# Two graph-attention layers and a transformer block on one core: first clips beside first values, ACT first at the values' banks, buffers of s moved, keys stacked inside SBUF, first rows loaded ahead of weights

## The chip, the cores and the metric

The kernel runs on one core of a Trainium2 chip. The metric is device time in microseconds (us); lower is better. Five runs of the kernel before gave a median of 3483.48 us (3477.29 to 3486.34).

The core's engines each take their instructions in a fixed order and wait for one another through semaphores: PE (matrix multiply; PEld is its weight load), DVE (vector), ACT (activation functions and copies), POOL (a second, slower vector engine) and SP, which here only issues transfers (DMA). The order on each engine is settled when the program is compiled.

## The reference, cut to what matters

There are 4096 rows of 256 features, 8 heads of 32, and a 4096x4096 adjacency matrix of int32.

```python
def _gat_layer(x, adj_mat, W, a):            # twice, each followed by elu(...) + input
    Wh = jnp.einsum('nd,hdo->hno', x, W)
    src = jnp.einsum('hno,ho->hn', Wh, a[:, :O])
    dst = jnp.einsum('hno,ho->hn', Wh, a[:, O:])
    e = jax.nn.leaky_relu(src[:, :, None] + dst[:, None, :], 0.2)
    e = jnp.where(adj_mat[None, :, :] > 0, e, NEG_INF)
    out = jnp.einsum('hnm,hmo->hno', jax.nn.softmax(e, axis=-1), Wh)
# then one transformer block with the same mask:
q, k, v = layer_norm(x) @ w_qkv              # split, 8 heads of 32
attn = softmax(where(adj != 0, q k^T * SCALE, -inf))
x = x + (attn v) @ w_proj + b_proj
x = x + gelu(layer_norm(x) @ w1 + b1) @ w2 + b2
```

## The kernel before, in words

**Graph attention** (`graph_attention`). exp(leaky_relu(s+d)) is either of two products of a row factor and a column factor, according to the sign of s+d. So the kernel only needs, per head, a 0/1 matrix "s >= -d" masked by the adjacency, and multiplies it by the values with their factors. The rows s are cut into 4 blocks of 1024. Work goes in 256 groups (layer, block of rows, pair of heads, group g of four 128-column tiles), 128 matmuls each at line 1302. For group i the loop over groups issues on PE the matmuls of group i, and beside them, at fractions of the group given by hand, the side steps of later groups:

- `compare(i + 2)`: eight comparisons of 128x1024, on DVE (line 1068) or on ACT (line 1066), then one AND with the mask on DVE (line 1073). The rows s come broadcast over the partitions in `s_b` (pool `g_s`, two buffers of 8 KB per partition), loaded by `s_fetch` (line 1049) from DRAM, where `term_rows` has put them (line 1019).
- For the mask of layer 0: `mask_load` fetches 512 KB of adjacency (line 855, three buffers), `mask_clip` turns it to fp8 on DVE (line 864, six buffers, and then issues the next load), `mask_turn` transposes it on PE (line 886), copies it out on ACT (line 888) and stores it (line 891).
- `preparation(l, q, bank)`: eleven steps for four tiles of values: two `features` (transposes at line 961, copies on ACT at line 964), then `values(t)` for t = 0 to 3, each followed one step later by `split(t - 1)`, and `term_rows`. `values` multiplies on PE (line 974) into a PSUM bank; DVE copies the 16 columns of terms (line 981); ACT takes two exponentials and a third one from that copy (lines 987, 988); DVE reduces (line 989), multiplies (line 995) into `g_prod` (two buffers) and scales (line 1001). `split` casts `g_prod` to f16 on ACT (line 1006) and POOL takes the remainder (line 1007).

Layer 0's eight preparations run in `begin()` (q = 0 and 1) and in groups 0 to 5; layer 1's run around groups 122 to 132. PE, ACT and DVE keep the written order inside this function (`manual_schedule`); SP's order is set by the planner. `begin()` runs preparation 0 and 1, with the first four clips beside q = 1, fetches s, then turns eight units and clips eight more, the last four of them for group 0's turns, and then compares for groups 0 and 1:

```python
        for q in range(2):
            for k, step in enumerate(preparation(0, q, spare_bank)):
                step()
                if q == 1 and k in (2, 4, 6, 8):
                    mask_clip(*units[k // 2 - 1])
```

**Pools.** A pool takes the addresses after those of the pools opened before it, and a pool opened after others are closed lies on their addresses and waits for whatever last used them. In order, after the masks (`g_mask`): `g_stage` 8 KB per partition, `g_rows` 26 KB, `g_t` 24 KB (the three compare buffers, read by the matmuls of line 1302 to the end), `g_s` 16 KB, `g_ep`. The transformer's pools lie on the same addresses: worked out from the tile sizes, counted from the end of `g_mask`, `u_mask` ends at 13 KB, `u_wq` is at 13 to 19 KB, `u_x` at 19 to 27, the layer norm's tiles (`u_ln`) at 27 to 37, its columns (`u_lnc`) at 37 to 45, the halves (`u_hv`) at 45 to 57.

**Queries, keys, values** (`unshifted_transformer`, line 1502). Eight blocks of 512 rows. `ready(nb)` loads rows (line 742) and normalises them (`normed`: mean on DVE at 1401, squares and a root on ACT at 1406 and 1410, rows on DVE at 1414); `turned` transposes them (PE line 1430, ACT line 1433). PE multiplies keys, then queries; ACT casts to f16 (line 1509), DVE takes the remainder (line 1510). The two halves go to `half_d` in DRAM in two stores (line 1514), and one block later come back in four loads (line 1455) as the stacked keys `u_k`, where partition group a of 32 holds half `order[a]` of head h in column h. Block 0's queries go the same way at once, those of later blocks while the attention runs. In this part all orders are the planner's, not written by hand.

**Attention** (lines 1554 to 1651) is scores on PE, exponential on ACT, mask on DVE, pair sums on POOL, and the products with values and ones on PE. Its last sums go through DRAM (`den_d`, `inv_d`, lines 1601 to 1623).

**Tail.** SP loads w_proj (line 1667), two row vectors (1671), w1 (1677) and w2 (1679), 1 MB each, and then `projected(0)` loads its rows (742) and its attention output (1692), adds the bias on POOL (1695), projects on PE (1699), adds on DVE (1706) and normalises. The feed-forward (1721, 1728, 1737) follows block by block, with `projected(nb + 1)` ahead of it.

Of the kernel before, what the change touches and what calls it, by code (L numbers as in the profile page):

```python
# [750 lines left out]
def graph_attention(  # L751
# [44 lines left out]
    mask_p = ctx.enter_context(tc.tile_pool(name="g_mask", bufs=10))  # L796
    stage_p = ctx.enter_context(tc.tile_pool(name="g_stage", bufs=2))
    rows_p = ctx.enter_context(tc.tile_pool(name="g_rows", bufs=2))
    t_p = ctx.enter_context(tc.tile_pool(name="g_t", bufs=3))
    s_p = ctx.enter_context(tc.tile_pool(name="g_s", bufs=2))  # L800
# [149 lines left out]
    def preparation(l, q, bank):  # L950
# [19 lines left out]
        def values(t):  # L970
# [10 lines left out]
            nc.vector.tensor_copy(  # L981
# [3 lines left out]
            big = some.tile([P, 2, H], F32, name="g_big")  # L985
            for i, scale in enumerate((-1.0, -LRELU)):
                nc.scalar.activation(big[:, i, :], L.negd[:, at, :], AF.Exp, scale=scale)
            nc.scalar.activation(L.r[:, at, :], L.terms[:, 0, at, :], AF.Exp, scale=LRELU - 1.0)
# [14 lines left out]
        def split(t):  # L1003
            part = held.pop(t).rearrange("p h i v -> p h (i v)")
            halves = vst[q][:, t].rearrange("p h (k v) -> p h k v", k=2)
            nc.scalar.copy(halves[:, :, 0, :], part)  # L1006
            nc.gpsimd.tensor_tensor(halves[:, :, 1, :], part, halves[:, :, 0, :], op=ALU.subtract)  # L1007
# [194 lines left out]
    def begin():  # L1202
# [5 lines left out]
        for q in range(2):  # L1208
            for k, step in enumerate(preparation(0, q, spare_bank)):
                step()  # L1210
                if q == 1 and k in (2, 4, 6, 8):
                    mask_clip(*units[k // 2 - 1])
        s_of[0, 0, 0] = s_fetch(0, 0, 0)
        for k, u in enumerate(units):
            mask_turn(*u)
            if k + 4 < len(units):
                mask_clip(*units[k + 4])
            else:
                mask_clip(*turns[0][k + 4 - len(units)])
# [110 lines left out]
def unshifted_transformer(  # L1330
# [42 lines left out]
    half_d = dram.tile([2, 2, DC, P, N], F16, name="half_d")  # L1373
# [69 lines left out]
    with ExitStack() as scope:  # L1443
# [7 lines left out]
        def stack(to, i, order, cols):  # L1451

            for a, kind in enumerate(order):
                first = half_d[i, kind, 0, 0:1, cols]
                nc.sync.dma_start(
                    to[a * O : (a + 1) * O],
                    spread(first, [[N, O], [O * N, DC * HC], [1, NB]]),
                )

        def load_queries(nb):  # L1460
            q_st = blocks.tile([P, DC * HC, NB], F16, name="u_q")
            stack(q_st, 0, (0, 1, 0, 1), slice(nb * NB, (nb + 1) * NB))
# [10 lines left out]
        with ExitStack() as qkv:  # L1473
# [16 lines left out]
            for nb in range(NNB):  # L1490
# [6 lines left out]
                for i in (1, 0):  # L1497
# [15 lines left out]
                    for kind in range(2):  # L1513
                        nc.sync.dma_start(
                            half_d[i, kind, :, :, cols].rearrange("c p n -> p c n"),
                            halves[:, kind],
                        )
# [11 lines left out]

                for b in (nb - 1,) if nb + 1 < NNB else (nb - 1, nb):  # L1530
                    if b >= 0:
                        at = slice(b * NB, (b + 1) * NB)
                        stack(k_st[:, :, at], 1, (0, 0, 1, 1), at)
                    if b == 0:
                        load_queries(0)
# [125 lines left out]
    with ExitStack() as scope:  # L1661
# [13 lines left out]
        b2_sb = by_row(b2, "u_b2")  # L1675
        w1_sb = big.tile([P, DC, F], F32, name="u_w1")
        nc.sync.dma_start(w1_sb, w1.rearrange("(c p) f -> p c f", p=P))
        w2_sb = big.tile([P, FC, D], F32, name="u_w2")
        nc.sync.dma_start(w2_sb, w2.rearrange("(c p) e -> p c e", p=P))
# [7 lines left out]
        def projected(nb):  # L1687

# [5 lines left out]
            )  # L1694
            nc.gpsimd.tensor_tensor(res, res, bp_sb, op=ALU.add)
# [15 lines left out]
        res, res_n = projected(0)  # L1711
        hn = turned(res_n, g2_sb, be2_sb, ln, ps_m)
        for nb in range(NNB):
            more = nb + 1 < NNB
            if more:
                res_next, res_n = projected(nb + 1)
# [115 lines left out]
```

## Time and profile before

| | us |
|---|---|
| median of five runs | 3483.48 |
| the profiled execution: its own time | 3481.72 |
| its span, first to last instruction | 3479.9 |
| start to the first matmul of group 0 | 61.35 |
| groups 0 to 5, about | 61 to 160 |
| layer 1's preparations, about | 896 to 975 |
| end of the last matmul of the graph attention | 1745.5 |
| first key matmul to first score matmul | 1761.87 to 1871.33 |
| end of the attention's last sums | 3185.6 |
| first feed-forward matmul | 3218.23 |

A line of the stage view gives, for a stretch of the span, its length, the busy time of each engine with the count of its instructions, the clock granted to PE as a share of full speed, the share of the DMA engines in use and GB/s. A line of the timeline gives start, length, engine, line, operation, output<-input and count; in brackets stands how long the engine was idle just before, and who ended that. A line of the waits gives the waiter, who released it, the total, the count and the longest. A line of one source line's instructions gives shortest/median/longest in ns. Times of consecutive instructions on DVE and ACT overlap by about 0.1 us, so that the step from one to the next is shorter than the length shown.

### The profile page before, as it was taken

The numbers are of one execution on the slowest core, as the hardware profiler recorded it, in microseconds if no ns is written. First come the engines' busy times: TensorE is split into PE (matmuls) and PEld (weight loads), VectorE is DVE, ScalarE is ACT, GpSimd is POOL, SyncE is SP. The second block draws the span as 40 slices with busy tenths as digits, with TensorE's granted clock in tenths as the row PEclk, the third lists the DMA queues.
The fourth block names the chain that finished last, engine by engine and source line by source line (L and its number), as shares of the span: only waits on it lengthen the run. The fifth ranks groups of instructions, "written<-read, shape, count | busy, mean of one in ns | idle before, by whom it ended". The sixth has DMA issues, their size and how long they took to land.

```text
span 3479.9 us, 97728 instructions
## 1 busy us (share of the span) xinstructions
PE 3299.2 (95%) x43156; PEld 2099.7 (60%) x43156; DVE 2882.0 (83%) x3250; ACT 2655.1 (76%) x3381; POOL 1323.1 (38%) x602
## 2 busy tenths in 40 slices
PE   4899999999889999999988999999999999997999
PEld 3799999999789999999953111111111111112666
DVE  6899999999779999999945999999999999996111
ACT  4799889988778888888855777777777777775332
POOL 1300000000210000000003999999999999996110
PEclk7999999999999999999989999999999999998999
DMA  6656545420311212121064010101011010002110
GB/s 203 189 183 203 157 152 163 142 81 27 96 51 39 74 47 87 39 75 39 13 177 113 19 31 19 32 25 25 25 26 37 13 44 10 26 10 67 44 47 26
DMA packets 214721, 250.57 MB, mean 72 GB/s; under 512 B 88528, under 2 KB 135632, under 8 KB 214288
## 3 DMA queue, kind: packets, MB, share of 16 engines
q1 hardware_dynamic: 214288, 244.25, 23.3%
q8 instruction: 339, 5.55, 0.6%
q14 instruction: 94, 0.77, 0.1%
HBM read 201.73 MB, written 42.47 MB: 70 GB/s over the span
## 4 chain that ended last, share of the span: by engine, by line
PE 39%; DVE 7%; ACT 4%; POOL 2%; DMA 1%; issue 1%; SPq 0%; DVEq 0%; ACTq 0%; POOLq 0%
PE u_ps L1554 12%; PE u_av L1568 12%; PE u_dn L1568 6%; DVE u_e L1563 4%; PE misc L1737 3%; PE bank L1302 2%; PE misc L1502 2%; POOL u_both L1651 2%; ACT u_ps L1561 1%; PE misc L1521 1%; PE misc L1721 1%; ACT ln_square L1406 1%; PE misc L1430 1%; DMA u_xres<-rows 1%; DVE t L1073 1%
## 5 line engine op out<-in xcount | busy, mean ns | idle before, releaser
L1302 PE MATMUL bank<-vst,t 128*128 128x66 f16 (+1 forms) x24576 | 1524.7, 203 | 47.4 <-DVE t L1073 39.9
L1302 PEld LDWEIGHTS <-t 128*128 128x128 fp8e4 x24576 | 1506.3, 97 | 66.6 <-DVE t L1073 48.5
L1302 PE MATMUL bank<-vst,mask 128*128 128x132 f16 x8192 | 1506.7, 222 | 0.0
L1066 ACT ACTIVATE t<-s_b,g_terms 128x1024 int8<-128x1024 f32 x1151 | 1243.5, 1164 | 99.2 <-PE bank L1302 94.7
L1651 POOL TENSOR_TENSOR u_both<-u_e 128x1024 f32<-128x1024 f32 x512 | 1199.9, 2366 | 233.1 <-DMA u_k<-half_d 126.4
L1563 DVE SCALAR_TENSOR_TENSOR u_e<-u_mask,u_ps 128x1024 f32<-128x1024 uint8 x1024 | 1202.4, 1217 | 88.5 <-ACT u_ps L1561 84.1
L1561 ACT ACTIVATE u_ps<-u_ps 128x1024 f32<-128x1024 f32 x1024 | 1010.9, 1008 | 281.4 <-PE u_ps L1554 262.4
L1302 PEld LDWEIGHTS <-mask 128*128 128x128 fp8e4 x8192 | 804.1, 98 | 0.0
L1073 DVE TENSOR_TENSOR t<-t,mask 128x2048 int32<-128x2048 int32 x256 | 589.9, 2304 | 110.7 <-ACT t L1066 89.3
L1068 DVE TENSOR_SCALAR t<-s_b,g_terms 128x1024 fp8e4<-128x1024 f32 x897 | 636.6, 754 | 0.0
L1554 PE MATMUL u_ps<-u_q,u_k 128*128 128x512 f16 x2048 | 579.6, 384 | 17.8 <-DVE u_e L1563 17.3
L1554 PEld LDWEIGHTS <-u_k 128*128 128x128 f16 x2048 | 139.2, 98 | 723.4 <-issue 664.3
L1568 PE MATMUL u_av<-u_e,u_v 128*32 128x512 f32 x4096 | 547.4, 606 | 0.0
L1007 POOL TENSOR_TENSOR vst<-g_prod,vst 128x528 f16<-128x528 f32 x64 | 83.9, 1321 | 937.8 <-ACT vst L1006 862.2
masks.py:197 POOL MEMSET u_ident<- 128x128 f32 x1 | 0.2, 205 | 727.5 <-ACT ln_square L1406 727.5
L1568 PE MATMUL u_dn<-u_both,u_ones 128*32 128x512 f32 x2048 | 274.1, 605 | 1.3 <-POOL u_both L1651 1.3
L1568 PEld LDWEIGHTS u_av<-u_e,u_v 128*32 128x32 f32 x4096 | 81.2, 108 | 219.1 <-issue 210.4
L1728 ACT ACTIVATE u_hid<-misc,u_b 128x512 f32<-128x512 f32 x64 | 42.3, 683 | 142.8 <-PE misc L1721 142.8
L1744 DVE TENSOR_TENSOR u_xres<-u_xres,misc 128x256 f32<-128x256 f32 x32 | 13.5, 421 | 122.7 <-PE misc L1737 122.7
L1737 PE MATMUL misc<-u_w,u_hid 128*128 128x256 f32 x512 | 111.8, 380 | 0.0
L1721 PE MATMUL misc<-ln_cols,u_w 128*128 128x512 f32 x256 | 111.2, 593 | 0.0
L864 DVE TENSOR_SCALAR adj<-g_adj 128x1024 fp8e4<-128x1024 int32 x128 | 97.2, 761 | 15.5 <-DMA g_adj<-in_adj_dram 15.5
(120 smaller groups left out, 1635.3 us busy)
## 6 DMA issues: line engine op xcount, KB each, us to landing
g_adj<-in_adj_dram SPq DMA_DIRECT2D x128, 512.0 KB
mask<-mask SPq DMA_DIRECT2D x128, 256.0 KB
s_b<-s_d SPq DMA_DIRECT2D x64, 512.0 KB
u_mask<-mask SPq DMA_DIRECT2D x32, 512.0 KB
mask<-stage SPq DMA_DIRECT2D x48, 256.0 KB
rows<-e_x SPq DMA_DIRECT2D x32, 256.0 KB
half_d<-u_halves SPq DMA_DIRECT2D x32, 256.0 KB
u_k<-half_d SPq DMA_DIRECT2D x32, 256.0 KB
```

Source lines behind the costliest of these rows:

```text
L864: nc.vector.tensor_scalar(v.rearrange("p m r -> p r m"), loaded.pop((nb, c, i)), 1.0, -(2.0**-30), op0=ALU.min, op1=ALU.max, saturate=False,)
L1066: nc.scalar.activation(to.bitcast(I8), s, AF.Sign, bias=negd, scale=-1.0)
L1068: nc.vector.tensor_scalar(to, s, negd, None, op0=ALU.is_ge, saturate=False)
L1073: nc.vector.tensor_tensor(both, both, m32.unsqueeze(1).to_broadcast(list(both.shape)), op=ALU.bitwise_and)
L1302: nc.tensor.matmul(to, left, right, start=k not in opened, stop=last)
L1554: nc.tensor.matmul(ps[:, j, :], k_st[:, h, mt * P : (mt + 1) * P], q_st[:, h, :], start=True, stop=True,)
L1561: nc.scalar.activation(ps, ps, AF.Exp, scale=SCALE)
L1563: nc.vector.scalar_tensor_tensor(e, mask, 0.0, ps, op0=ALU.not_equal, op1=ALU.mult)
L1568: nc.tensor.matmul(to[j * O : (j + 1) * O, :], lefts[j], es[j // 2][:, j % 2, :], start=start, stop=stop,)
L1651: nc.gpsimd.tensor_tensor(both, es_of[i - 1][u], es_of[i][u], op=ALU.add)
L1721: nc.tensor.matmul(ph, w1_sb[:, k, f * P : (f + 1) * P], hn[:, k, :], start=(k == 0), stop=(k == DC - 1),)
L1737: nc.tensor.matmul(po[:, :D], hid[:, f, at : at + P], w2_sb[:, f, :], start=(f == 0), stop=(f == FC - 1),)
```

## The change

Five edits:

1. `begin()`: clips of units 0 to 3 stand beside q = 0 (after steps 3, 5, 7, 9), clips of units 4 to 7 and the turns of units 0 to 2 beside q = 1; what follows turns units 3 to 7 and clips the four units of group 0.
2. `values` and `split`: the copy of the terms goes from DVE to ACT; the three exponentials read the PSUM bank and not the copy; `g_big` has four buffers; the cast in `split` goes from ACT to DVE.
3. The pool `g_s` is opened ahead of `g_stage`. Counted again from the end of `g_mask`: `g_s` 0 to 16 KB, `g_stage` 16 to 24, `g_rows` 24 to 50, `g_t` 50 to 74.
4. The halves of the keys, and of block 0's queries, go from SBUF to the stacked tile in SBUF, 16 transfers of 64 KB each per block (`stacked`), with no store to DRAM and no load from it. Later queries still go through `half_d`.
5. In the tail the rows and the attention output of block 0 are loaded before the second row vector, w1 and w2, and w_proj's tile is allocated after the first row vector.

```diff
     mask_p = ctx.enter_context(tc.tile_pool(name="g_mask", bufs=10))
+    s_p = ctx.enter_context(tc.tile_pool(name="g_s", bufs=2))
     stage_p = ctx.enter_context(tc.tile_pool(name="g_stage", bufs=2))
     rows_p = ctx.enter_context(tc.tile_pool(name="g_rows", bufs=2))
     t_p = ctx.enter_context(tc.tile_pool(name="g_t", bufs=3))
-    s_p = ctx.enter_context(tc.tile_pool(name="g_s", bufs=2))
...
-            nc.vector.tensor_copy(
+            nc.scalar.copy(
                 L.terms[:, :, at, :], pv[:, D : D + 2 * H].rearrange("p (k h) -> p k h", k=2)
             )
-            big = some.tile([P, 2, H], F32, name="g_big")
+            big = some.tile([P, 2, H], F32, name="g_big", bufs=4)
             for i, scale in enumerate((-1.0, -LRELU)):
-                nc.scalar.activation(big[:, i, :], L.negd[:, at, :], AF.Exp, scale=scale)
-            nc.scalar.activation(L.r[:, at, :], L.terms[:, 0, at, :], AF.Exp, scale=LRELU - 1.0)
+                nc.scalar.activation(big[:, i, :], pv[:, D + H : D + 2 * H], AF.Exp, scale=scale)
+            nc.scalar.activation(L.r[:, at, :], pv[:, D : D + H], AF.Exp, scale=LRELU - 1.0)
...
-            nc.scalar.copy(halves[:, :, 0, :], part)
+            nc.vector.tensor_copy(halves[:, :, 0, :], part)
             nc.gpsimd.tensor_tensor(halves[:, :, 1, :], part, halves[:, :, 0, :], op=ALU.subtract)
...
             for k, step in enumerate(preparation(0, q, spare_bank)):
                 step()
+                if q == 0 and k in (3, 5, 7, 9):
+                    mask_clip(*units[(k - 3) // 2])
                 if q == 1 and k in (2, 4, 6, 8):
-                    mask_clip(*units[k // 2 - 1])
+                    if k > 2:
+                        mask_turn(*units[k // 2 - 2])
+                    mask_clip(*units[k // 2 + 3])
         s_of[0, 0, 0] = s_fetch(0, 0, 0)
-        for k, u in enumerate(units):
-            mask_turn(*u)
-            if k + 4 < len(units):
-                mask_clip(*units[k + 4])
-            else:
-                mask_clip(*turns[0][k + 4 - len(units)])
+        for k in range(3, len(units)):
+            mask_turn(*units[k])
+            if k - 3 < len(turns[0]):
+                mask_clip(*turns[0][k - 3])
...
+        def stacked(to, halves, order):
+            for a, kind in enumerate(order):
+                by_chunk = to[a * O : (a + 1) * O].rearrange("p (c j) n -> p c j n", c=DC)
+                for j in range(HC):
+                    nc.sync.dma_start(by_chunk[:, :, j, :], halves[j * O : (j + 1) * O, kind])
...
-                    for kind in range(2):
-                        nc.sync.dma_start(
-                            half_d[i, kind, :, :, cols].rearrange("c p n -> p c n"),
-                            halves[:, kind],
-                        )
+                    if i == 1:
+                        stacked(k_st[:, :, cols], halves, (0, 0, 1, 1))
+                    elif nb == 0:
+                        load_queries(0, halves)
+                    else:
+                        for kind in range(2):
+                            nc.sync.dma_start(
+                                half_d[kind, :, :, cols].rearrange("c p n -> p c n"),
+                                halves[:, kind],
+                            )
...
-                for b in (nb - 1,) if nb + 1 < NNB else (nb - 1, nb):
-                    if b >= 0:
-                        at = slice(b * NB, (b + 1) * NB)
-                        stack(k_st[:, :, at], 1, (0, 0, 1, 1), at)
-                    if b == 0:
-                        load_queries(0)
...
         bp_sb = by_row(b_proj, "u_bp")
-        b2_sb = by_row(b2, "u_b2")
-        w1_sb = big.tile([P, DC, F], F32, name="u_w1")
-        nc.sync.dma_start(w1_sb, w1.rearrange("(c p) f -> p c f", p=P))
-        w2_sb = big.tile([P, FC, D], F32, name="u_w2")
-        nc.sync.dma_start(w2_sb, w2.rearrange("(c p) e -> p c e", p=P))
+        wp_sb = big.tile([P, DC, D], F32, name="u_wp")
+        nc.sync.dma_start(wp_sb, w_proj.rearrange("(c p) e -> p c e", p=P))
...
-        res, res_n = projected(0)
+        first = rows_of(0)
+        b2_sb = by_row(b2, "u_b2")
+        w1_sb = big.tile([P, DC, F], F32, name="u_w1")
+        nc.sync.dma_start(w1_sb, w1.rearrange("(c p) f -> p c f", p=P))
+        w2_sb = big.tile([P, FC, D], F32, name="u_w2")
+        nc.sync.dma_start(w2_sb, w2.rearrange("(c p) e -> p c e", p=P))
+        res, res_n = projected(*first)
```

`rows_of(nb)` holds the two loads that stood at the head of `projected`; later blocks call it just before `projected`.

## The prediction

> **What bounds the kernel now.** I read the page first, then a table of stages, then the waits and the timeline of the stages that the change touches.
>
> ```profile
> PE 3299.2 (95%) x43156; PEld 2099.7 (60%) x43156; DVE 2882.0 (83%) x3250; ACT 2655.1 (76%) x3381; POOL 1323.1 (38%) x602
> ```
>
> 95% of PE means that the long stages leave little. What can be won lies at the seams, so the next view is the table of stages (length, busy time per engine, clock, DMA share, GB/s):
>
> ```profile
> 0.00:61.30 61.30, 18.99 (x84) 13.68 (x84) 32.10 (x71) 24.57 (x56) 10.76 (x16) 0.73 0.72 226
> 61.30:160.00 98.70, 78.57 (x1038) 67.64 (x1039) 79.95 (x148) 67.43 (x164) 31.13 (x23) 0.96 0.54 168
> 896.00:975.00 79.00, 65.46 (x910) 56.97 (x911) 59.67 (x115) 57.66 (x142) 28.50 (x23) 0.98 0.31 96
> 1745.40:1761.90 16.50, 4.25 (x21) 3.17 (x18) 13.04 (x30) 12.32 (x29) 0.60 (x2) 0.60 0.67 208
> 1761.90:1871.30 109.40, 97.20 (x305) 57.32 (x305) 37.62 (x74) 54.50 (x132) 0.00 (x0) 0.92 0.64 170
> 3182.00:3218.20 36.20, 15.31 (x52) 10.72 (x49) 7.87 (x20) 7.88 (x15) 9.55 (x5) 0.67 0.49 160
> ```
>
> PE idles 42 us at the start, 20 and 14 in the two stretches of preparations, 12 at the change of layers, 12 in the key stage, 21 before the feed-forward. Every edit aims at one of these. Who ends the idle time, from the timeline (start, length, engine, line; in brackets the idle time before):
>
> ```profile
> 48.17 0.70 DVE L864 TENSOR_SCALAR adj<-g_adj 128x1024 fp8e4<-128x1024 int32 x1 [7.04 <-DMA g_adj<-in_adj_dram]
> 54.89 0.70 DVE L864 TENSOR_SCALAR adj<-g_adj 128x1024 fp8e4<-128x1024 int32 x1 [2.77 <-DMA g_adj<-in_adj_dram]
> 79.59 1.64 DVE L864 TENSOR_SCALAR adj<-g_adj 128x1024 fp8e4<-128x1024 int32 x1
> 89.27 0.69 DVE L995 TENSOR_TENSOR g_prod<-turn,g_big 128x512 f32<-128x512 f32 x1 [0.76 <-POOL vst L1007]
> 96.82 2.29 DVE L1073 TENSOR_TENSOR t<-t,mask 128x2048 int32<-128x2048 int32 x1 [1.25 <-ACT t L1066]
> 1745.51 1.22 DVE L1401 TENSOR_REDUCE ln_mean<-u_x 128x4 f32<-128x1024 f32 x1 [7.50 <-PE bank L1302]
> 1759.89 2.19 PE L1430 MATMUL misc<-u_ident,ln_rows 128*128 128x128 f32 x8 [3.68 <-DVE ln_rows L1414]
> 1811.75 2.19 PE L1430 MATMUL misc<-u_ident,ln_rows 128*128 128x128 f32 x8 [3.92 <-DVE ln_rows L1414]
> 3192.29 0.51 SPq L1692 DMA_DIRECT2D u_att<-att_d  x1
> 3197.92 6.04 PE L1699 MATMUL misc<-u_wp,u_att 128*128 128x256 f32 x16 [12.32 <-DMA u_att<-att_d]
> ```
>
> **Edit 1, clips.** A load needs the buffer of the third clip before it. Before, the first clip runs at 24.34, so DMA lies idle from 16 to 23 us, and clips 8 to 11 (counted from 0) wait for loads at 48.17 to 55.6; only then DVE does its five comparisons (3.4) and the AND (2.29): group 0 at 61.35. Now the first clip follows the second tile of values, at about 16.1. I follow DVE from 13.1 with steps of 1.0 for a tile, 0.6 for a clip, 0.35 for a cast and a wait for POOL (1.15 a tile) where `g_prod`'s two buffers are full: q = 0 ends at 25, q = 1 at 38, clip 8 runs at 39. Load 11, freed by it, took 6.0 before (issued about 48.9, clipped 54.89): clip 11 at 45.3, then 0.7 + 3.4 + 2.3: group 0 at 51.5. **-10 us.** Ends: the slowest load of this stretch (issue 39.26, clip 48.17: 8.9) with a slower DVE gives -5; no POOL waits gives -15. The fetch of s (8.4 from issue to landing) is no later: its terms now come from ACT, and it lands some 5 us ahead of clip 11. It is what is late next.
>
> **Edit 2, values.** Per group before, 16.4 us in layer 0 (83.34 to 99.70) and 13.4 in layer 1, set by DVE and ACT in turns. DVE loses four copies (0.09 each, start to start) and gains four casts of 128x528. No such cast is in the trace: ends are 0.35 (128x512 at 0.42, line 937, starts overlapping) and 0.63 (128x512 at 0.69, line 995); I take 0.35, since the 128x1024 comparison with one SBUF source also runs at that pace (0.75). So +1.0. ACT loses four casts (0.62) and gains four copies (0.17 to 0.25, as lines 988 and 1016): the wait at the AND goes (1.25 in layer 0; 0, 1.24, 2.49, 2.94 in layer 1, mean 1.7), with 0.17 in front of three products; PE's late banks (0.6 twice in layer 0) go about half. New: POOL now starts behind DVE's own cast, two steps before the next product needs the buffer: 0.8 and 0.9 of waiting instead of 0.76 (layer 0) and of 0.97 + 0.62 (layer 1). Sum: about -0.4 for 6 groups, -0.5 for 8: **-6 us.** Ends: casts at 0.63 add 14 x 4 x 0.28 = 16, so +10; no POOL waits at all, -17. The four `g_big` buffers are hidden: ACT runs at most that far ahead.
>
> A row speaks against this edit: the clip of 79.59 took 1.64, not 0.69, beside a POOL instruction, and POOL's own took 1.60, not 1.15. The Trainium skill, "SBUF — State Buffer", section "Who interferes with whom", has a rule for it: a cast or tensor_scalar in a two-port mode and a GpSimd instruction exclude each other for a whole instruction, while ScalarE never waits. By that rule at its worst each of the four casts brings one full POOL instruction into DVE's line, 4.6 per group where 2.7 are lost now; the sum of all edits would be -5 instead of -32.
>
> **Edit 3, places.** The layer norm's tiles lie at 27 to 37 KB: over `g_t`, read by the last matmul, before; over `g_rows`, long free, after. That is the 7.50 at 1745.51: DVE and ACT were idle from 1738. Now mean and squares of blocks 0 and 1 (2 x 1.2 on DVE, 2 x 2.5 on ACT) fit ahead of 1746. What stays: the constants (`u_eps`, g1, be1) lie over `g_keep`, last read by DVE at 1750.5 (line 1112); with no mean in its way that read ends at about 1749.2. Root, rows (1.4 a block), turns (2.2 a block, cold): keys start at about 1754.5 instead of 1761.87. **-7 us**; ends -11 (constants hidden too) and +2 (the planner leaves the means behind the GAT's tail). `u_wq` now waits for s, free at 1735; its 768 KB have 19 us. Without that cover it would cost its 3 to 4 us.
>
> **Edit 4, keys.** The trip through DRAM ends on no path: block 0's last load is issued at 1784.9, and scores start at 1871.33, 0.46 behind the copy of the last values. So 0 from the transfers. SP: 16 issues a block instead of 6. Nearest rows:
>
> ```profile
> L1455 SPq DMA_DIRECT2D u_k<-half_d x32: 444/462/493, 1772.6 to 1872.7; - x32
> L1514 SPq DMA_DIRECT2D half_d<-u_halves x32: 359/360/467, 1769.9 to 1868.8; - x32
> ```
>
> Issue to issue is 0.28 (line 1601, four in 1.12) to 0.50: 4.5 to 8.0 a block; with two query stores, rows and mask (1.7) at most 9.7, under the 11.2 of an unstalled block (1786.15 to 1797.35). Hidden. Block 0 has 32, 16 us at most: behind them the rows of block 4, now landed by 1775 and turned at 1796, would land at about 1787, and they need some 8 us to be normalised; it just fits. PE's stalls before blocks 5, 6 and 7 (3.92 each, plus 2.5 of slow clock) come from DVE's order: the mean at 1805.64 stands behind four remainders though its rows were issued at 1797.0. The planner may move it either way, 19 us for three blocks; nearest row: as before, 0.
>
> Against small transfers: the Trainium skill, "DMA: Bandwidth & Descriptors", section "Bandwidth", calls transfers under 64 KB descriptor-dominated and gives 0.95 us for 64 KB; sixteen in a row would be an estimated 15 us per block and PE would wait 4, which makes the sum about 0.
>
> **Edit 5, tail.** Before, SP meets the rows after w1, w2 and the wait for the sums (issue 3191.8), and `u_att` lands at 3197.8 among 2 MB of weights. After: four issues from 3182.0, done at 3183.9; 1.4 MB at the 0.3 to 0.38 MB/us of the start: 3188.5. **-9 us.** Ends: PE still warm (line 1699 takes 3.62 at 3246.65, not 6.04): -12; DVE's reciprocal of the sums (waiting until 3195.1) ordered ahead of the projections' additions: -2. The weights have from 3185 to 3209; what is late next is that chain of sums.
>
> **Sum.** -10 - 6 - 7 + 0 - 9 = -32. The profiled execution took 3481.7 (span 3479.9, 1.8 around it), so 3449.7; it lies 1.8 under the median, so **3451**.
>
> **Rivals.**
> - *The planner also frees blocks 5 to 7* (or most of edit 2's upper gain comes): 3451 - 19 = **3432**. For it: half a megabyte less traffic a block. Against: nothing in the diff moves the mean. 0.18.
> - *DVE becomes the bound of the preparations*: +10 in place of -6: **3467**. For it: the 1.64 and 1.60 rows. Against: DVE waits 2 to 4 us a group now. 0.17.
> - *The seams do not come*: the change doesn't do there what it says, because the planner keeps the old order (edits 3 and 5 give 0 and -2): **3465**. Against: both waits name a transfer or a buffer that is moved. 0.10.
> - *SP becomes the bound of the key stage.* 16 transfers at p plus 1.7 a block: the gains are eaten where a block takes (109.4 + 32) / 8 = 17.7, p = 1.0 us. At 1.13, the pitch of the four stores of line 1514 with their waits (4.52): 19.8 x 8 - 109.4 = +49, so **3500**. 0.07.
> - My forecast: 0.48; its own range is 3440 to 3462.
>
> 0.2%, about what a measurement can tell here, is 7 us. Faster: nearly all of the first four cases, 0.87; same 0.05 (DVE's bound with a stall or two); slower 0.08. The range 3426 to 3474 leaves out the SP case and the far end of the two before it.
>
> **What would show it.** Right: group 0's first matmul near 51; no clip waiting 7 us; the AND of a preparing group without a wait for ACT; the first mean ahead of the last matmul of the graph attention, and the first key matmul 9 us behind that matmul's end, not 16.4; 16 issues a block with SP idle between; the projection's 12.3 us wait down to about 3. Wrong: casts of 1 us or more on DVE; rows landing late in blocks 2 to 4; DVE's reciprocal ahead of the additions of line 1706.

## The result and the profile after

The changed kernel takes 3490.0 us (median of 23 runs, 3485.9 to 3494.2), the kernel before 3482.06 in the same comparisons: ratio 1.0022, 95% interval 1.0017 to 1.0028. It is slower by about 8 us, where 32 us less were forecast. The profiled execution took 3493.64, with a span of 3491.8. Line numbers are now each kernel's own: in the changed one they stand 2 to 17 higher from the main loop on.

The page of the changed kernel shows PE as busy as before, and ACT's work moved to DVE (2882.0 to 2904.6, ACT 2655.1 to 2622.7):

```profile
PE 3297.4 (94%) x43156; PEld 2100.3 (60%) x43156; DVE 2904.6 (83%) x3250; ACT 2622.7 (75%) x3381; POOL 1329.3 (38%) x602
```

The stages of the changed kernel, in the columns of the stage view: the start, layer 1's preparations, a stretch in the middle of layer 1 that was even before, the seam behind the graph attention, the key stage, the tail.

```profile
0.00:53.10 53.10, 17.19 (x85) 12.47 (x86) 32.36 (x71) 17.31 (x54) 12.17 (x16) 0.78 0.79 247
896.00:975.00 79.00, 66.04 (x969) 59.29 (x968) 68.64 (x119) 48.61 (x130) 29.96 (x20) 0.94 0.27 83
1213.00:1232.00 19.00, 11.86 (x208) 11.28 (x206) 9.22 (x11) 10.01 (x21) 0.00 (x0) 0.79 0.28 93
1748.40:1759.50 11.10, 2.54 (x10) 1.91 (x11) 9.12 (x24) 7.44 (x12) 0.60 (x2) 0.72 0.78 229
1759.50:1883.20 123.70, 98.04 (x313) 58.23 (x311) 39.26 (x76) 54.44 (x132) 0.00 (x0) 0.89 0.49 127
3198.30:3230.00 31.70, 15.93 (x53) 11.15 (x50) 9.46 (x20) 7.88 (x15) 9.53 (x5) 0.68 0.61 192
```

The start is 8 us shorter, the seam 5 and the tail 4, as planned in kind. The key stage is 14 longer with the same work on PE (98.04 against 97.20), and PE has a hole of 7 us near 1220, in a stretch where it did not wait at all before.

To see where each microsecond goes, I lined up the 256 AND instructions of the graph attention (DVE, line 1073, one per group), the first key matmul, the first score matmul, the start of the last pair sums on POOL and the end. After minus before, in us, in the two profiled executions:

| up to | running difference | step |
|---|---|---|
| AND of group 0 | -8.3 | -8.3 |
| AND of group 122 (layer 0's preparations done) | -10.1 | -1.8 |
| AND of group 160 (layer 1's preparations done) | -7.8 | +2.3 |
| AND of the last group | +2.5 | **+10.2** |
| first key matmul | -2.3 | -4.8 |
| first score matmul | +11.9 | **+14.2** |
| start of the last pair sums | +16.3 | **+4.4** |
| end | +11.9 | -4.4 |

Three steps lose (the +2.3 is taken up under no_values). The lines behind them, from the timeline of DVE of the changed kernel:

```profile
34.50 1.38 DVE L1006 CAST vst<-g_prod 128x528 f16<-128x528 f32 x1
45.61 0.75 DVE L1068 TENSOR_SCALAR t<-s_b,g_terms 128x1024 fp8e4<-128x1024 f32 x1 [3.64 <-DMA s_b<-s_d]
...
1221.68 1.22 DVE L1403 TENSOR_REDUCE ln_mean<-u_x 128x4 f32<-128x1024 f32 x1 [6.18 <-DMA u_x<-rows]
1229.74 2.29 DVE L1073 TENSOR_TENSOR t<-t,mask 128x2048 int32<-128x2048 int32 x1 [3.46 <-ACT t L1066]
...
1890.83 5.74 DVE L1573 SCALAR_TENSOR_TENSOR u_e<-u_mask,u_ps 128x1024 f32<-128x1024 uint8 x5 [7.78 <-DMA half_d<-u_halves]
```

and from that of PE:

```profile
1808.87 2.10 PE L1432 MATMUL misc<-u_ident,ln_rows 128*128 128x128 f32 x8 [13.84 <-DVE ln_rows L1416]
...
3208.07 6.70 PE L1709 MATMUL misc<-u_wp,u_att 128*128 128x256 f32 x16 [6.18 <-DMA u_att<-att_d]
```

The clips no longer wait; what is late at the start is now s (45.61). At 1221.68 stands the layer norm's first mean, the transformer's work in the middle of the graph attention: DVE waits 6.18 us for its rows, and group 169's AND is late by 9.1. At 1808.87 PE has waited 13.84 for block 4 (3.92 was the longest stall of the stage before). At 1890.83, 7.6 us behind the first score matmul, DVE's first product of the attention waits for a transfer; in the kernel before it waited for the exponential and came 3.0 behind:

```profile
1874.33 5.75 DVE L1563 SCALAR_TENSOR_TENSOR u_e<-u_mask,u_ps 128x1024 f32<-128x1024 uint8 x5 [5.56 <-ACT u_ps L1561]
```

SP's timeline of the changed kernel shows why block 4 is late (start, length from first to last issue, count):

```profile
1766.40 10.40 SPq L1467 DMA_DIRECT2D u_k<-u_halves  x16
1776.90 10.22 SPq L1467 DMA_DIRECT2D u_q<-u_halves  x16
1787.21 10.22 SPq L1467 DMA_DIRECT2D u_k<-u_halves  x16
1797.53 1.07 SPq L1531 DMA_DIRECT2D half_d<-u_halves  x2
1798.65 0.49 SPq L742 DMA_DIRECT2D u_x<-rows  x1
```

Sixteen issues take 10.2 us, 0.64 each, and 48 of them stand ahead of block 4's rows, which go out at 1798.65. In the kernel before they went out 28 us earlier:

```profile
1770.37 0.41 SPq L742 DMA_DIRECT2D u_x<-rows  x1
```

### The profile page after: what moved, and what is told of

Read it like the earlier page. It is cut to its first block, busy times and chain, and to the rows that moved or that the text cites. A ratio compares the mean times of both kernels' runs of the same rounds, so it can differ in the third digit from the quotient of the medians.

```text
span 3491.8 us, 97827 instructions
## 1 busy us (share of the span) xinstructions
PE 3297.4 (94%) x43156; PEld 2100.3 (60%) x43156; DVE 2904.6 (83%) x3250; ACT 2622.7 (75%) x3381; POOL 1329.3 (38%) x602
## 4 chain that ended last, share of the span: by engine, by line
PE 38%; DVE 7%; ACT 4%; POOL 2%; DMA 2%; issue 1%; SPq 1%; DVEq 0%; ACTq 0%; POOLq 0%
PE u_ps L1564 12%; PE u_av L1578 11%; PE u_dn L1578 6%; DVE u_e L1573 4%; PE misc L1754 3%; PE bank L1304 2%; POOL u_both L1661 2%; ACT u_ps L1571 1%; PE misc L1514 1%; SPq L1467 1%; ACT ln_square L1408 1%; PE misc L1738 1%; PE misc L1432 1%; DMA u_xres<-rows 1%; DVE t L1073 1%
## 5 line engine op out<-in xcount | busy, mean ns | idle before, releaser
L1310 ACT COPY ev_broad<-bank 128x396 f32<-128x396 f32 x192 | 89.1, 472 | 24.9 <-PE bank L1304 21.3
```

## The experiments

Ratios are against the kernel before, in the same comparison, with 95% intervals. Markers are those of the table above; "stage" is first key matmul to first score matmul, and "attention" is from there to the start of the last pair sums.

| kernel | median us | ratio | stage | attention |
|---|---|---|---|---|
| no_keys | 3480.87 | 0.9990 (0.9981 to 0.9999) | 117.0 | 1309.0 |
| no_places | 3490.15 | 1.0021 (1.0012 to 1.0030) | 123.6 | 1313.1 |
| no_values | 3492.93 | 1.0028 (1.0017 to 1.0038) | 123.8 | 1313.5 |
| keys_alone | 3502.91 | 1.0055 (1.0041 to 1.0069) | 124.0 | 1313.2 |
| starts_and_tail | 3469.34 | 0.9964 (0.9953 to 0.9975) | 109.3 | 1308.8 |
| keys_pool_queue | 3463.19 | 0.9947 (0.9934 to 0.9961) | 99.9 | 1312.5 |
| keys_32_transfers | 3563.65 | 1.0236 (1.0222 to 1.0250) | 181.9 | 1326.6 |
| s_behind_rows | 3476.63 | 0.9983 (0.9974 to 0.9992) | 116.7 | 1308.7 |
| pool_queue_no_places | 3465.01 | 0.9956 (0.9944 to 0.9968) | 93.4 | 1314.7 |
| pool_queue_s_behind | 3463.75 | 0.9953 (0.9939 to 0.9966) | 100.9 | 1313.1 |
| rows_pool_queue | 3485.67 | 1.0013 (1.0005 to 1.0022) | 109.3 | 1317.6 |
| pool_queue_tail | 3464.23 | 0.9954 (0.9942 to 0.9966) | 95.6 | 1313.8 |
| halves_moved | 3490.88 | 1.0018 (1.0009 to 1.0028) | 124.1 | 1313.2 |
| pool_queue_halves_moved | 3466.28 | 0.9952 (0.9938 to 0.9965) | 99.2 | 1313.0 |
| pool_queue_np_halves_moved | 3462.27 | 0.9942 (0.9929 to 0.9956) | 93.4 | 1314.8 |
| last_block_two_queues | 3462.07 | 0.9939 (0.9926 to 0.9953) | 94.2 | 1313.0 |
| two_queues | 3456.70 | 0.9923 (0.9909 to 0.9936) | 91.5 | 1308.6 |

### One edit undone, one edit alone

**no_keys**: `half_d` in two stores and four loads a block again.

```diff
-                        stacked(k_st[:, :, cols], halves, (0, 0, 1, 1))
...
+                        stack(k_st[:, :, at], 1, (0, 0, 1, 1), at)
```

> All edits but edit 4: keys and first queries go through DRAM again. Theory (SP bounds the key stage: 16 issues in 10.2 us, 0.64 each, where 4.5 to 8.0 us were reckoned): first key matmul to first score falls from 123.7 to about 109.5 us, the 4 us of stalls at the attention's first steps go, and the time is about 3490 - 18.6 = 3471. Rival (the key stage is late because the weights of the queries and the constants come later now, edit 3's doing): the stage stays near 120 us and the time near 3488.

9 us less than the changed kernel, where 18.6 less were expected. The stalls at the attention's start went, but the stage fell only to 117.0. With edit 3 the planner leaves block 4's rows behind the key transfers even here:

```profile
1782.74 0.45 SPq L742 DMA_DIRECT2D u_x<-rows  x1
```

That line of SP is 12 us behind its place in the kernel before, and PE has four stalls of 3.92 in the stage, not three. Why the planner does so with edit 3's places is not shown.

**no_places**: the old order of the pools.

```diff
-    s_p = ctx.enter_context(tc.tile_pool(name="g_s", bufs=2))
     stage_p = ctx.enter_context(tc.tile_pool(name="g_stage", bufs=2))
     rows_p = ctx.enter_context(tc.tile_pool(name="g_rows", bufs=2))
     t_p = ctx.enter_context(tc.tile_pool(name="g_t", bufs=3))
+    s_p = ctx.enter_context(tc.tile_pool(name="g_s", bufs=2))
```

> All edits but edit 3: the pool of s is opened last again. Theory (the freed places let the planner put the layer norm's first mean into the middle of the graph attention, at 1221.7 us, where DVE waits 6.2 for its rows and 10.6 us are lost; at the seam edit 3 gives back 5.1): the mean goes back behind the last matmul, the step between 1220 and 1280 us vanishes, the time is about 3490 - 10.6 + 5.1 = 3484.5. Rival (the planner's order there comes from the other edits, since it orders the program anew): the mean stays near 1220, only the seam gets worse, about 3495.

The theory's mechanism is there: DVE's timeline has the first mean behind the last matmul again, and from the AND of group 160 to that of 180 it takes 121.0 us and not 131.3.

```profile
1737.16 1.22 DVE L1403 TENSOR_REDUCE ln_mean<-u_x 128x4 f32<-128x1024 f32 x1 [7.85 <-PE bank L1304]
```

The time did not fall: 3490.15. The profiled executions differ by 5.3 us (spans 3486.5 and 3491.8), the medians by nothing. Over all kernels here, 160 to 180 takes 121.0 to 122.0 us without edit 3 and 126.6 to 131.9 with it (mean 129.5 of eight), and the seam (last AND to first key matmul) 26.1 to 26.5 with the old order and 21.3 with edit 3's. So edit 3 loses 8 and gains 5 there, about 3 net, which the medians of this pair are too coarse to show.

**no_values**: edit 2 undone as a whole: the engines of `values` and `split`, what the exponentials read and the buffers of `g_big` as before. The two moved instructions:

```diff
-            nc.scalar.copy(
+            nc.vector.tensor_copy(
                 L.terms[:, :, at, :], pv[:, D : D + 2 * H].rearrange("p (k h) -> p k h", k=2)
...
-            nc.vector.tensor_copy(halves[:, :, 0, :], part)
+            nc.scalar.copy(halves[:, :, 0, :], part)
```

> All edits but edit 2: ACT casts again, DVE copies the terms again. Theory (edit 2 gains 1.8 us in layer 0's groups and loses 2.3 in layer 1's): the time is within 3 us of 3490, layer 1's preparations some 2 us shorter and layer 0's some 2 us longer. Rival 1 (the casts make DVE the bound of the preparations, +10 as in the prediction's second rival): 3480. Rival 2 (edit 2 gains the 6 us that were predicted, and something else in the groups hides it): 3496.

3 us slower than with edit 2, at the edge of what the intervals tell apart; the traces say where. The steps from group 0's AND to group 9's take 114.45 us with edit 2 (mean of 16 kernels) and 116.65 without (mean of 3); layer 1's preparations, group 122 to 140, take 181.5 and 181.4. Single executions scatter by 4 us there, so the +2.3 of the table above is within the scatter.

**keys_alone**: the kernel before with edit 4's lines of the diff and nothing else.

> The kernel before with edit 4 alone. Theory (SP bounds the key stage by itself): about 3482 + 18.6 = 3501, with the 16 issues of a block at 10.2 us and PE waiting for the rows of block 4. Rival (edit 4 costs nothing alone, it only collides with the later weights and constants of edit 3): 3482.

+19.8 us, as the theory had it: stage +14.6, attention +4.7. Edit 4 alone makes the loss, and it makes the same one on top of edits 1, 2 and 5: no_places (3490.15) differs from starts_and_tail (3469.34, next) by edit 4 alone.

**starts_and_tail**: the kernel before with the lines of edits 1, 2 and 5.

> Edits 1, 2 and 5 alone (places and keys as before). Theory (edits 3 and 4 together take all that the others give; edit 3 costs 7 us in a stall at group 169, gives 5 at the seam and takes 7 in the key stage, because the rows of block 4 are issued at 1782.7 us behind the key transfers and not at 1770.4): group 0 starts 8 us early, no stall near 1220, the key stage takes 109.5 us again, the tail gives 2.5 to 4.6: about 3483 - 13 = 3470. Rival (the order of the key stage changes with any edit, so the stage stays at 117 us): 3477.

3469.34: theory. Against no_keys (3480.87), which has edit 3 besides, it says that edit 3 costs 9 to 11.5 where edit 4 is not there (by the ratios and by the medians). The stage has the length and clock of the kernel before, in its stage line:

```profile
1755.00:1864.30 109.30, 97.07 (x306) 57.28 (x306) 37.73 (x74) 54.64 (x132) 0.00 (x0) 0.92 0.65 171
```

### What an issue costs, and who pays it

**keys_32_transfers**: each transfer cut in two.

```diff
-                    nc.sync.dma_start(by_chunk[:, :, j, :], halves[j * O : (j + 1) * O, kind])
+                    for c in range(DC):
+                        nc.sync.dma_start(by_chunk[:, c, j, :], halves[j * O : (j + 1) * O, kind, c, :])
```

> The changed kernel with each stacked transfer of 64 KB cut into two of 32 KB, 32 a block. Theory (SP pays 0.64 us for each issue, whatever its size): 20.5 us a block, the stage is set by SP at about 41 + 7 x 22 = 195 us, the time about 3490 + 70 = 3560. Rival (the pitch is the time of the bytes, about 102 bytes a ns with the share of DMA at 0.45): the pitch falls to 0.32 and the time stays at 3490.

3563.65 for 3560. SP's timeline keeps 0.63 to 0.64 an issue at half the bytes, so the rival, a pitch set by the bytes, is out:

```profile
1781.32 20.16 SPq L1468 DMA_DIRECT2D u_q<-u_halves  x32
```

**keys_pool_queue**: POOL issues what `stacked` moves.

```diff
-                    nc.sync.dma_start(by_chunk[:, :, j, :], halves[j * O : (j + 1) * O, kind])
+                    nc.gpsimd.dma_start(by_chunk[:, :, j, :], halves[j * O : (j + 1) * O, kind])
```

> The changed kernel with the stacked transfers issued by POOL, which does nothing else in the key stage. Theory (what costs is that they stand in SP's line ahead of the rows of block 4): the rows are issued before 1785 us, PE's stall of 13.84 us falls to about 4, the key stage takes 110 to 117 us and the time is 3474 to 3483. Rival (the transfers themselves are slow, whoever issues them, and the halves' buffers come free late): the stage stays near 123 us and the time near 3490.

27 us faster than the change and 11 below the fast end of the expectation. PE's timeline has one stall in front of a block, and POOL's shows 0.53 an issue:

```profile
1798.23 8.77 PE L1514 MATMUL misc<-ln_cols,u_wq 128*128 128x512 f32 x16 [5.01 <-ACT u_v L1545]
```

```profile
1854.17 8.42 POOL L1467 DMA_DIRECT2D u_k<-u_halves  x16 [3.84 <-ACT u_v L1545]
```

The three stalls before blocks 5 to 7 that the kernel before had are gone too. SP, with neither key loads nor stacked transfers, issues the last rows at 1787.1 instead of 1826.2.

**rows_pool_queue**: the stacked transfers stay on SP.

```diff
-                rows.load(xs, nb * TB)
+                rows.load(xs, nb * TB, by=nc.gpsimd)
```

> The changed kernel with its 16 stacked transfers per block still on SP, but the rows of the layer norm issued by POOL. Theory (the loss is the rows' place in SP's line, and behind it SP's own 10.2 us a block): PE's stall of 13.84 us goes, SP's line alone sets the end of the stage (20.6 + 7 x 11.3 us from 1766 on, so the last keys are issued near 1866 instead of 1886.9), the stage takes about 107 us and the time is about 3474. Rival (the order of the rows matters little, the halves' buffers that SP frees late set the pace): 3488.

The stage is near the expectation (109.3 for 107; PE's longest stall in front of a block is 5.07), the time is not: 4 us less than the change by the medians, 7 by the traces. The traces find 4.7 us of what is missing at the attention's first product, which waits longer than in the change:

```profile
1883.02 5.75 DVE L1573 SCALAR_TENSOR_TENSOR u_e<-u_mask,u_ps 128x1024 f32<-128x1024 uint8 x5 [12.19 <-DMA half_d<-u_halves]
```

Another 1.8 lie in layer 1's preparations, within the scatter there; the stretch of group 169 is the same as in the change (160 to 180: 131.9 against 131.3). SP's last sixteen are issued from 1868.5 to 1878.7. With no long wait left in the middle, SP's own line, some 11.5 to 12 us a block, sets when the stage's last transfer goes out.

### Places

**s_behind_rows** has edits 1, 2, 5 and another order of the pools; **pool_queue_s_behind** has the stacked transfers on POOL's queue besides, and **pool_queue_no_places** the same with the old order of the pools.

```diff
+    rows_p = ctx.enter_context(tc.tile_pool(name="g_rows", bufs=2))
     s_p = ctx.enter_context(tc.tile_pool(name="g_s", bufs=2))
     stage_p = ctx.enter_context(tc.tile_pool(name="g_stage", bufs=2))
-    rows_p = ctx.enter_context(tc.tile_pool(name="g_rows", bufs=2))
```

> Edits 1, 2, 5 and another order of the pools in place of edit 3: rows, s, stage, t. The layer norm's tiles lie over s, free at about 1734, and not over rows, free since about 1000. Theory (the freed places let the planner put the first means at 1220): now they can't start before 1734, the stall of 7 us at group 169 is gone, and the time is about 3480.9 - 7.3 = 3473.5 or, if block 4's rows are early too, 3467. Rival (the planner puts them there for another reason, or the stall is another's): the stall stays and the time is 3481.

> As the run before, with the order of pools rows, s, stage, t. Theory: no stall in the groups (7 us less than with edit 3's order) and the seam's gain kept, since the means of blocks 0 and 1 run behind the last comparisons near 1734 us: 3463.2 - 7 = 3456. Rival (with s in its way the layer norm is late again and the seam loses what the groups give): 3461 or more.

> Edits 1, 2, 5 and the stacked transfers on POOL's queue; places as before (edit 3 undone). Theory (edit 3 nets a loss by itself: about 7 us in the stall at group 169, about 5 given back at the seam): the stall goes, the first key matmul stands some 7 us closer to the start than in the kernel before, the key stage stays at 100 us, the time is 3463.2 - 2 = 3461. Rival (edit 3 is what lets the key stage run in 100 us, with its rows and weights early): the stage goes back to 109 and the time to about 3470.

In all three the stall near 1220 is gone (160 to 180: 121.0, 121.0 and 121.6), so it was the freed place that let the mean in. The first came 3 us above the expectation, with block 4's rows late again (stage 116.7). The other two missed by 8 and 4. In pool_queue_s_behind the rival was right: the seam takes 25.1 us where edit 3's order has 21.3, which is 3.8 of the 6.9 us that the groups gain on keys_pool_queue. In pool_queue_no_places the seam is back at 26.5; its stage is 6.5 shorter than in keys_pool_queue (93.4), of which the attention gives back 2.2 (1314.7 against 1312.5). The traces say 3.8 us less than keys_pool_queue where the medians say 1.8 more, so the rest is not settled. With the keys on another queue, edit 3 makes no difference that these runs can tell: 3463.2 and 3466.3 with it, 3465.0 and 3462.3 without.

### The attention's first product

**halves_moved**, **pool_queue_halves_moved**, **pool_queue_np_halves_moved**: a gap of 20 KB ahead of the halves' pool. Worked out from the tile sizes, the ten buffers of `u_e`, 40 KB from where `u_wq` began, reach into the halves without the gap and end ahead of them with it.

```diff
+            gap = qkv.enter_context(tc.tile_pool(name="u_gap", bufs=1))
+            gap.tile([P, 20, 256], F32, name="u_gap")
             hv = qkv.enter_context(tc.tile_pool(name="u_hv", bufs=3))
```

> The changed kernel with a gap of 20 KB per partition ahead of the halves' pool, so that the first tiles of the attention no longer lie over it. Theory (DVE's first product of the attention waits 7.78 us for the last transfers that read the halves): that wait goes, the attention's end stands 1308.5 us behind its first score, as in the kernel before, and not 1312.9: about 3490 - 4.4 = 3485.6. Rival (the last keys land late, and PE or ACT would wait for them anyway): 3490.

> The changed kernel with the transfers on POOL's queue and the same gap. Theory: the wait of the first products goes, the stretch from first score to the attention's end falls from 1312.5 to about 1308.5: 3463.2 - 4 = 3459. Rival (the last keys): 3463.

> The same with edit 3 undone. Theory (the stretch was 1314.7 there, the wait of the first product 9.86 us): 3465 - 6 = 3459, equal to the run with edit 3 within 3 us, since what edit 3 loses in the groups it gives back at the seam. Rival 1 (edit 3's stall near 1220 counts in full once the wait is gone): 5 us or more below the run with edit 3. Rival 2 (the last keys): 3465.

My theory of the overlap fell: nothing moved (1313.2, 1313.0, 1314.8), and DVE still waits, in halves_moved:

```profile
1891.96 5.75 DVE L1575 SCALAR_TENSOR_TENSOR u_e<-u_mask,u_ps 128x1024 f32<-128x1024 uint8 x5 [7.95 <-DMA half_d<-u_halves]
```

The new theory: the product waits for the last transfer that reads the halves, wherever they lie. In the traces DVE waits for eight semaphores ahead of this one product, in the changed kernel as in halves_moved (for four in the kernel before), and behind it for ACT's alone. I read this so: the first instruction that writes into the pool opened behind the closed ones takes over the waits for all their transfers. No run shows that reading by itself.

**last_block_two_queues**, **two_queues**: of the last block's transfers, or of all, SP issues every second one; edits 1, 2, 5 besides. The edit of two_queues, against pool_queue_no_places:

```diff
-                    nc.gpsimd.dma_start(by_chunk[:, :, j, :], halves[j * O : (j + 1) * O, kind])
+                    (nc.sync if j % 2 else nc.gpsimd).dma_start(
+                        by_chunk[:, :, j, :], halves[j * O : (j + 1) * O, kind]
+                    )
```

> As pool_queue_no_places (edits 1, 2, 5 and the stacked transfers on POOL's queue), but of the last block's 16 transfers SP issues every second one. Theory (the first product of the attention waits for the last transfer that reads the halves): the last 16 take about 5 us from first to last issue instead of 8.41, the first product starts about 7 us behind the first of them and not 10.1, and the time falls by 3: 3465 - 3 = 3462. Rival (that wait is for something else that ends then, such as the last queries' way through DRAM): the first product stays where it was, 3465.

> The same with SP issuing every second one of all 16 transfers in every block. Theory (8 issues of 0.64 us and the two stores, 6.2 us a block, leave SP's line free, and POOL's 8 take 4.2): the key stage stays at 93 to 100 us, the first product comes 3 us earlier: 3462. Rival (SP's line again delays the rows of block 4, by up to 10 us in block 0 with its 32 transfers): PE stalls 4 us or more there, 3467.

The first: 3462.07 for 3462, with DVE's product at

```profile
1856.17 5.74 DVE L1578 SCALAR_TENSOR_TENSOR u_e<-u_mask,u_ps 128x1024 f32<-128x1024 uint8 x5 [7.78 <-DMA half_d<-u_halves]
```

It comes 7.6 us behind the first score matmul (1848.54), where it came 9.7 behind it in pool_queue_no_places: 2 of the 3 us. The last transfer is now the last queries' store, which SP issues behind its eight. It reads the halves too, so here the rival's case (the last queries' way through DRAM) is one of the theory's, and this run doesn't part the two. The second kernel is the fastest of all, 3456.70, 5 below its expectation. Its stage line:

```profile
1755.90:1847.30 91.40, 89.57 (x305) 53.92 (x305) 36.76 (x74) 52.93 (x132) 38.31 (x72) 0.98 0.69 180
```

SP's timeline, with the rows of blocks 4 and 5 behind 24 issues instead of 48:

```profile
1762.54 5.29 SPq L1467 DMA_DIRECT2D u_k<-u_halves  x8
...
1779.47 1.11 SPq L742 DMA_DIRECT2D u_x<-rows  x2
```

and DVE's:

```profile
1850.33 5.74 DVE L1575 SCALAR_TENSOR_TENSOR u_e<-u_mask,u_ps 128x1024 f32<-128x1024 uint8 x5 [5.56 <-ACT u_ps L1573]
```

PE works 89.57 of 91.40 us at a clock of 0.98. The first product waits for the exponential, 5.56 us, as in the kernel before, and the attention takes 1308.6. With the last transfer early the 4 us are gone, and moving the halves did nothing: their cause is the last transfer of the stage. All 19 kernels agree: beyond the 1308.5 us of the kernel before, the attention is longer by as much as its first product lags more than 3.0 us behind the first score, within 0.7.

### The tail

**pool_queue_tail**: pool_queue_s_behind with block 0's rows and attention output issued by ACT.

```diff
-        first = rows_of(0)
+        first = rows_of(0, nc.scalar)
```

> As the run with the order rows, s, stage, t and POOL's queue, and block 0's rows and attention output in the tail issued by ACT instead of SP. Theory (edit 5 stops short because the planner leaves the attention output behind the stores of the last sums, issued 8.2 us behind the start of the last pair sums; behind that stands DVE's reciprocal): the projection starts 4 us earlier behind the attention's end, but its additions still stand behind the reciprocal, so the time falls by only 1 to 2: 3454.5. Rival (the additions aren't held by the reciprocal): 4 less, 3452.

No change (3464.23 against 3463.75), and the projection starts 15.8 us behind the start of the last pair sums, not 12.2. PE's timeline shows another transfer in place of the one removed, a second load of the whole of w_proj:

```profile
3170.32 0.40 SPq L1686 DMA_DIRECT2D u_wp<-in_L_gnn_w_proj_dram  x1
3176.88 6.53 PE L1709 MATMUL misc<-u_wp,u_att 128*128 128x256 f32 x16 [10.03 <-DMA u_wp<-in_L_gnn_w_proj_dram]
```

Every kernel with edit 5 loads w_proj twice. The edit adds the later tile and its load (line 1686), but the earlier ones stay (line 1677, issued at 3163.28 here), and no matmul reads what they load. So w_proj's tile is not moved behind the first row vector, as the change says, but doubled, and here the projection waits for the copy that SP issues behind the stores of the sums. No run is without the second load; what it costs the other kernels is open.

## Why the prediction was wrong, point by point

**The step that failed is edit 4's zero**, and in it the sentences "Hidden. Block 0 has 32, 16 us at most: behind them the rows of block 4 [...] would land at about 1787 [...]; it just fits." The price of an issue was 0.64 us, not 0.28 to 0.50: those rows were issues of other transfers, and I took their spread for both ends of an unknown. And 48 issues stand ahead of block 4's rows, not 32: block 1's keys are ahead of them too. 48 x 0.64 = 30.7 us, from 1766.4 to 1797.5. Measured: 0 predicted, +19.8 alone. In the change 14.2 of it are in the key stage. The other 4.4 have no term in the prediction at all: it said that the trip ends on no path and put 0 for the transfers, but the attention's first product waits for the last of the new ones.

- The rival *SP becomes the bound of the key stage* was the right mechanism in the wrong place. I let it decide from p = 1.0 us, where SP is slower than PE in every block. It decides far earlier, at the first blocks, through what stands behind the transfers in SP's line, and at the end, through what waits for the last one.
- The rule weighed there (the Trainium skill, "DMA: Bandwidth & Descriptors", section "Bandwidth") pointed the right way, with an estimated 15 us a block; 10.2 were measured. That the figures are near each other is luck: the page's 0.95 us is the time of a load from HBM, 0.64 that of an issue, and the issue did not follow the size, 64 KB and 32 KB cost the same. The same page's section "Issuing engines are not separate DMA queues" says that issuing from several engines saves only the issuing time, usually small beside the transfer. Here that time was what counted: two_queues takes 33 us off no_places, which differs from it by the queue alone.
- The rival *the planner also frees blocks 5 to 7* at -19 came true where SP was relieved: the stage is 18 us shorter in two_queues than before (91.5 against 109.5). I had put its cause in the traffic. What the traces show is that the rows of blocks 4 to 7 are all issued by 1795 us, where the last went out at 1826 before, and that the planner's order on DVE is another; no run parts these causes.

**Edit 3, -7.** Its seam was -5 (mean and squares are ahead, the constants are late as foretold). What I did not see: a place that is free since about 1000 us lets the planner put the mean wherever its rows are, into the middle of an engine's written order, where DVE, ACT and then PE wait for that load. +8 there, and in no_keys, without edit 4, +7.7 more in the stage by block 4's rows. My other end, "the planner leaves the means behind", looked only one way.

**Edit 1, -10.** Right in mechanism, -6.4 in size: group 0's AND at 52.25 without edit 2, against 59.0 and 58.2 without both (51.2 with both, mean of 16). Its first matmul came at 53.08 and not at 51.5. The fetch of s, which I had 5 us early, ends the stretch: 3.64 us of waiting at 45.61.

**Edit 2, -6.** About -3, the limit of what these runs tell apart: 1.0 at the start and 2.2 in layer 0's groups. In layer 1 (DVE, group 118 to 134, no_values and the change) the wait for ACT's comparisons fell as foretold, from 15.1 us to 3.6, and that for PE's banks from 6.8 to 0; in their place came waits for ACT's exponentials (7.2 instead of 2.4), for POOL (13.1 instead of 10.9) and the casts themselves. DVE's busy time in the 79 us rose from 59.67 to 68.64, and nothing was gained. Casts that a POOL instruction held up were few: 3 of 64 took 1.38 us, the others 0.43. The rival with DVE as the bound was wrong in size, and what spoke for it, instructions slowed beside POOL, was rare among the casts.

**Edit 5, -9.** -4: 295.7 us from the start of the last pair sums to the end, 300.1 and 299.1 without it. With the edit 15 of 17 kernels take 294.5 to 296.6; pool_queue_tail takes 298.3, and two_queues 300.5 in its one trace, 3.4 of it more than in the change behind DVE's last instruction. The projection starts 6 earlier, not 9, since the planner issues `u_att`, and the second load of w_proj just ahead of it, behind the stores of the sums, and DVE's first addition stands behind the reciprocal, the lower end that was named.

The sum by the measured sizes: -6.4 - 3.2 + 3 + 18.6 - 4 = +8.0, with edit 4 at its steps in the change (14.2 + 4.4). The medians say +8. Each part is good to 1 to 3 us, so that they meet this closely is luck.

## What to carry to other kernels

Price the issue of a transfer by itself, on the queue that will carry it, and ask what stands behind it in that queue's line: a queue can be harmless in its total and still hold back one load by 28 us. An edit that frees a buffer early hands the planner a freedom, so ask what may move there and what it would wait for. When removing a trip costs time, try the same transfers on an idle queue before giving the idea up: here it turned 8 us more than before into 19 less, and on two queues, with edit 3 undone, into 27 less.

## What was not expected of the hardware

- An issue of an SBUF to SBUF transfer costs 0.64 us on SP, at 64 KB as at 32 KB, and 0.53 on POOL at 64 KB, while loads of 256 KB from DRAM go out every 0.50 us on SP. Why the former is dearer was not settled.
- During those issues (1766.4 to 1797.5 in the change) the DMA engines are at a share of 0.43 and PE is granted its full clock: nothing in a stage line looks loaded. Only the queue's own timeline shows it.
- Executions of one and the same code differ by 2.3 us in 116 in layer 0's groups (118.15 against 115.81, keys_alone and the kernel before), so a step of that size in one pair of traces means nothing.
